# Batch statistics from per-sample moments and a Gram matrix, worked on as 39x39 tables and spread over the partitions by masked matmuls

## Chip, cores, metric

One core of one Trainium2 chip. The metric is device time in microseconds (us), the slowest core of a run, lower is better. Each time is a median over four or five runs. A verdict of "faster" or "slower" needs 2%.

In the lines of the profile PE is TensorE (matmuls) and PEld its weight loads, DVE is VectorE, ACT ScalarE, POOL GpSimd and SP SyncE; a q behind a name is the engine's queue of instructions, L139 is line 139 of that run's kernel, and x4 counts instructions. SBUF and PSUM are on-chip memories; the matmuls here write to PSUM. A load is issued by an engine's queue and has landed when its data is there. Cuts are marked with "...".

## The reference

Shortened (the last two lines leave out reshapes):

```python
B, F0, F1, E, C = (256, 39, 39, 16, 1)          # the inputs really have 1024 samples
rows, cols = np.tril_indices(39, k=-1)          # 741 pairs, col < row
cross = xj[:, rows, :, None] * xi[:, cols, None, :]            # [1024, 741, 16, 16]
mean = jnp.mean(cross, axis=(0, 2, 3), keepdims=True)          # one number a pair
var = jnp.mean(jnp.square(cross - mean), axis=(0, 2, 3), keepdims=True)
normed = (cross - mean) * jax.lax.rsqrt(var + 1e-05) * gamma + beta
out = normed[:, :, None] * W                                   # 777 MB of float32
```

The output takes nearly all the time. The statistics, two numbers for each of 741 pairs, must be known before the first output row.

## The kernel before

The batch lies on the partitions (128 x 8 samples). Mean and variance of each field over E are taken per sample; then all 741 pair products are formed per sample and averaged over the batch by matmuls with a matrix of ones, which also leaves the result on every partition.

```python
for t0 in range(0, NT, TS):                      # TS = 2, NT = 8
    for x, m, v in ((xj_sb, ma, va), (xi_sb, mb, vb)):
        nc.vector.tensor_reduce(ms[:, :, :, 0], xs, AX.X, ALU.add)
        nc.vector.tensor_scalar_mul(ms, ms, 1.0 / E)
        nc.vector.tensor_tensor(dev, xs, ms.to_broadcast([P, TS, F, E]), ALU.subtract)
        nc.scalar.activation(dev, dev, AF.Square)
        nc.vector.tensor_reduce(vs[:, :, :, 0], dev, AX.X, ALU.add)
        # ... scale
q_c = pairs(nc.gpsimd, va, sb, "q_c")            # 38 instructions each, [128, 8, 741] in all
q_a = pairs(nc.vector, ma, mb, "q_a")
batch_mean(ps_m, [q_a], True, True)              # matmuls of 371 and 370 columns
q_b = pairs(nc.vector, sa, vb, "q_b")
batch_mean(ps_v, [q_b, q_c], True, False)
# ... (q_a - mean) ** 2, batch_mean once more, then rsqrt, s and t on [128, 741]
```

The product loop that follows is the same text in both kernels:

```python
for r in order:                                  # 1, 38, 2, 37, ... 
    for t0 in range(0, NT, nt):
        nc.gpsimd.tensor_tensor(xs, xi_sb[...], s_sb[...], ALU.mult)
        # y = xs (outer) xj: VectorE for r <= 6, else 16 ScalarE activations a sample
        # y = (y + t) * W: one VectorE scalar_tensor_tensor a pair
        nc.sync.dma_start(out_v[...], y)
```

## Time and profile before

| | before | changed |
|---|---|---|
| time, first measurement | 3103.19 us | 3065.15 us |
| time, second measurement of both, in one job | 3101.28 us | 3062.89 us |
| first outer product on ScalarE (Z), first profile | 115.56 us | 76.07 us |
| first outer product, second profile | 114.25 us | 75.81 us |
| loop from Z to the end, second profile | 2984.55 us | 2985.09 us |

Z is the moment where the statistics end for the loop; the span minus Z is the loop.

### The profile page before, as it was taken

The page shows a single profiled execution, that of the slowest core. Times are in us where ns is not written, and L with a number is a line of the kernel's source. Part 1 is how long each engine was busy: PE and PEld are TensorE (multiplying, and loading weights), DVE is VectorE, ACT ScalarE, POOL GpSimd, SP SyncE. Part 2 cuts the span into 40 slices and gives each one's busy share as a digit, 9 for nine tenths or more (in the row PEclk, how much of TensorE's full clock was granted, in tenths as well). Part 3 has the DMA queues.
Part 4 walks back from the last instruction along what each step waited for, and adds up shares of the span by engine and source line. Part 5 has one row for each costly group of instructions (what it writes and reads, how often), then busy time and mean ns, then how long its engine had stood idle before and what let it go on. Part 6 is the DMA issues. An engine that isn't in the chain of part 4 may idle for free.

```text
span 3100.0 us, 10969 instructions
## 1 busy us (share of the span) xinstructions
PE 45.6 (1%) x128; PEld 26.7 (1%) x128; DVE 2448.0 (79%) x5253; ACT 2015.7 (65%) x4117; POOL 1659.1 (54%) x252
## 2 busy tenths in 40 slices
PE   2300000000000000000000000000000000000000
PEld 1100000000000000000000000000000000000000
DVE  8687888888888787777777787768777777778786
ACT  2446455464635777777676767676868686868685
POOL 2375757665666656555646464646363636362623
PEclk9655555555555555555555555555555555555555
DMA  2165656566555656666656656565656565666666
GB/s 78 78 265 228 282 244 259 250 269 271 250 252 248 293 237 281 256 268 268 288 249 263 265 240 272 246 281 242 270 243 281 244 281 249 276 263 268 275 267 275
DMA packets 43653, 783.71 MB, mean 253 GB/s; under 512 B 3472, under 2 KB 4496, under 8 KB 11824
## 3 DMA queue, kind: packets, MB, share of 16 engines
q1 hardware_dynamic: 42784, 779.56, 59.1%
q10 hardware_dynamic: 576, 2.56, 0.2%
q0 software_dynamic: 208, 0.89, 0.1%
q14 instruction: 84, 0.69, 0.1%
q8 instruction: 1, 0.02, 0.0%
HBM read 6.00 MB, written 776.99 MB: 253 GB/s over the span
## 4 chain that ended last, share of the span: by engine, by line
ACT 48%; POOL 45%; DVE 3%; issue 2%; PE 1%; DMA 0%; POOLq 0%; DVEq 0%; ACTq 0%
ACT y L183 48%; POOL xs L166 45%; PE ps_v L111 1%; DVE y L191 1%; DVE q_a L100 1%; DVE dev L86 0%; PE ps_m L111 0%; DMA xj_sb<-in_r_xj_dram 0%; DVE ma L83 0%; DVE vb L88 0%; DVE va L88 0%; DVE mb L83 0%; DVE inv L140 0%; DVE rstd L146 0%; DVE inv L144 0%
## 5 line engine op out<-in xcount | busy, mean ns | idle before, releaser
L191 DVE SCALAR_TENSOR_TENSOR y<-y,t_sb,w_sb 128x256 f32<-128x256 f32 (+2 forms) x5068 | 2314.6, 534 | 610.3 <-ACT y L183 610.1
L183 ACT ACTIVATE y<-xs,xj_sb 128x608 f32<-128x608 f32 (+31 forms) x4096 | 1994.9, 580 | 978.7 <-POOL xs L166 978.7
L166 POOL TENSOR_TENSOR xs<-xi_sb,s_sb 128x576 f32<-128x576 f32 (+19 forms) x206 | 1637.3, 7958 | 1368.8 <-ACT y L183 1315.6
L175 DVE TENSOR_TENSOR y<-xs,xj_sb 128x256 f32<-128x256 f32 (+5 forms) x48 | 51.5, 1136 | 1.5 <-POOL xs L166 1.4
L100 POOL TENSOR_TENSOR q_c<-va,sb 128x8 f32<-128x8 f32 (+37 forms) x38 | 19.6, 553 | 39.3 <-DVE sb L93 39.3
L87 ACT ACTIVATE dev<-dev 128x1248 f32<-128x1248 f32 x8 | 9.9, 1243 | 26.1 <-DVE dev L86 25.9
L129 ACT COPY mean<-ps_m 128x371 f32<-128x371 f32 (+1 forms) x2 | 0.9, 468 | 31.0 <-PE ps_m L111 31.0
L138 DVE TENSOR_SCALAR var<-ps_v 128x371 f32<-128x371 f32 (+1 forms) x2 | 1.1, 545 | 22.1 <-PE ps_v L111 22.0
L100 DVE TENSOR_TENSOR q_a<-ma,mb 128x8 f32<-128x8 f32 (+37 forms) x38 | 18.2, 554 | 0.0
L142 ACT ACTIVATE rstd<-inv 128x741 f32<-128x741 f32 x1 | 0.8, 822 | 25.9 <-DVE inv L140 25.9
L111 PE MATMUL ps_m<-q_a,ones 128*128 128x371 f32 (+1 forms) x32 | 15.7, 662 | 56.1 <-DVE q_a L100 56.1
L83 DVE TENSOR_REDUCE ma<-xj_sb 128x78 f32<-128x1248 f32 x4 | 5.8, 1452 | 6.9 <-DMA xj_sb<-in_r_xj_dram 6.9
L111 PE MATMUL ps_v<-q_a,ones 128*128 128x371 f32 (+1 forms) x32 | 10.2, 474 | 0.0
L111 PE MATMUL ps_v<-q_b,ones 128*128 128x371 f32 (+1 forms) x32 | 10.2, 474 | 0.0
L111 PE MATMUL ps_v<-q_c,ones 128*128 128x371 f32 (+1 forms) x32 | 10.1, 474 | 0.0
L100 DVE TENSOR_TENSOR q_b<-sa,vb 128x8 f32<-128x8 f32 (+37 forms) x38 | 9.9, 341 | 0.0
L111 PEld LDWEIGHTS ps_m<-q_a,ones 128*128 128x128 f32 x32 | 8.5, 274 | 62.7 <-issue 57.0
L131 DVE TENSOR_TENSOR q_a<-q_a,mean 128x741 f32<-128x741 f32 x8 | 6.8, 925 | 1.6 <-ACT mean L129 1.6
L132 ACT ACTIVATE q_a<-q_a 128x741 f32<-128x741 f32 x8 | 6.6, 822 | 1.1 <-DVE q_a L131 1.0
L111 PEld LDWEIGHTS ps_v<-q_a,ones 128*128 128x128 f32 x32 | 6.1, 189 | 3.9
L111 PEld LDWEIGHTS ps_v<-q_c,ones 128*128 128x128 f32 x32 | 6.1, 189 | 3.9
L111 PEld LDWEIGHTS ps_v<-q_b,ones 128*128 128x128 f32 x32 | 6.1, 189 | 3.9
(30 smaller groups left out, 49.6 us busy)
## 6 DMA issues: line engine op xcount, KB each, us to landing
out_dram<-y SPq DMA_DIRECT2D x14, 4608.0 KB, 12.4
out_dram<-y SPq DMA_DIRECT2D x15, 4096.0 KB, 11.2
out_dram<-y SPq DMA_DIRECT2D x12, 4864.0 KB, 12.9
out_dram<-y SPq DMA_DIRECT2D x12, 4352.0 KB, 11.8
out_dram<-y SPq DMA_DIRECT2D x14, 3584.0 KB, 10.0
out_dram<-y SPq DMA_DIRECT2D x15, 3072.0 KB, 8.8
out_dram<-y SPq DMA_DIRECT2D x12, 3840.0 KB, 10.6
out_dram<-y SPq DMA_DIRECT2D x12, 3328.0 KB, 9.3
```

The source lines that it names most:

```text
L83: nc.vector.tensor_reduce(ms[:, :, :, 0], xs, AX.X, ALU.add)
L87: nc.scalar.activation(dev, dev, AF.Square)
L100: engine.tensor_tensor(q[:, :, first[r] : first[r] + r], rows[:, :, r : r + 1].to_broadcast([P, NT, r]), cols[:, :, 0:r], ALU.mult,)
L111: nc.tensor.matmul(acc[:, : n1 - n0], ones, q[:, t, n0:n1], start=start and k == 0, stop=stop and k == len(qs) * NT - 1,)
L129: nc.scalar.copy(mean[:, 0, n0:n1], acc[:, : n1 - n0])
L131: nc.vector.tensor_sub(q_a[:, t], q_a[:, t], mean[:, 0])
L132: nc.scalar.activation(q_a[:, t], q_a[:, t], AF.Square)
L138: nc.vector.tensor_scalar_add(var[:, n0:n1], acc[:, : n1 - n0], BN_EPS)
L166: nc.gpsimd.tensor_tensor(xs, xi_sb[:, t0 : t0 + nt, 0:r, :], s_sb[:, :, n0 : n0 + r, :].to_broadcast([P, nt, r, E]), ALU.mult,)
L175: nc.vector.tensor_tensor(y[:, t], xs[:, t].unsqueeze(2).to_broadcast([P, r, E, E]), xj_sb[:, t0 + t, r : r + 1, :].unsqueeze(3).to_broadc ...
L183: nc.scalar.activation(y[:, t, :, i, :], xs[:, t], AF.Copy, scale=xj_sb[:, t0 + t, r, i : i + 1],)
L191: nc.vector.scalar_tensor_tensor(y2[:, :, c, :], y2[:, :, c, :], t_sb[:, n0 + c : n0 + c + 1], w_sb.to_broadcast([P, nt, EE]), ALU.add, AL ...
```

## The change

The intent is to make the statistics stage short: fewer matmul columns, arithmetic on 39x39 tables instead of 128x741, and subtracts shared with GpSimd. It takes per-sample sums of each field, and squares about a common shift (the field's mean over 256 samples, two of the eight on each partition), so that nothing large cancels. A Gram matrix by matmul then gives every pair's moments at once. Cut to its core:

```diff
-        nc.gpsimd.dma_start(g_sb, gamma.partition_broadcast(P))
-        nc.gpsimd.dma_start(b_sb, beta.partition_broadcast(P))
+        for r in range(1, F):                       # 38 + 38 loads of 4 to 152 bytes
+            nc.sync.dma_start(g_sq[r : r + 1, 0:r], gamma[n0 : n0 + r].unsqueeze(0))
+            nc.scalar.dma_start(b_sq[r : r + 1, 0:r], beta[n0 : n0 + r].unsqueeze(0))
+        def shifts():   # matmul of the first sums with ones, then
+            nc.scalar.activation(shift..., ps_s[:, 0 : 2 * F], AF.Copy, scale=k_s)
+        def squares(t0):
+                engine = nc.vector if (t0, x) in DEV_ON_VECTOR else nc.gpsimd   # 3 of 8 on VectorE
+                engine.tensor_tensor(dev, src[...], shift..., ALU.subtract)
+                nc.scalar.activation(dev, dev, AF.Square, scale=0.25)
+                nc.vector.tensor_reduce(to, dev, AX.X, ALU.add)
+                nc.vector.scalar_tensor_tensor(to, total[...], 1.0 / E, shift..., ALU.mult, ALU.subtract)
+        def gram(t0):
+            for t in range(t0, t0 + TS):
+                for acc, lhs in zip(ps_g, (fa[:, t, 0], fa[:, t, 1], ones[:, 0:F])):
+                    nc.tensor.matmul(acc[0:F, 0 : 2 * F + 1], lhs, fb[:, t], ...)
-        (114 pair products, three batch means, all arithmetic on [128, 741])
+        (22 instructions on [39, 39] tables, giving stq = s and t)
+        for r0, r1 in ROW_GROUPS:                   # 7 groups of up to 6 rows
+            nc.vector.tensor_tensor(wide, stq (n times), eye[:, r0:r1], ALU.mult)   # [39, n * 78]
+            nc.tensor.matmul(ps, ones[0:F, :], wide, start=True, stop=True)
+            for r in range(r0, r1):
+                nc.scalar.copy(st_sb[:, :, first[r] : first[r] + r], ps[:, r - r0, :, 0:r])
```

More of the change, by code (lines that the diff above doesn't have):

```diff
@@ L15 @@
 VECTOR_ROW = 6
+DEV_ON_VECTOR = ((2, 1), (4, 1), (6, 1))
+ROW_GROUPS = ((1, 7), (33, 39), (7, 13), (27, 33), (13, 19), (21, 27), (19, 21))
 @with_exitstack
@@ L43, in tile_pair_outer_batchnorm @@
     NP = F * (F - 1) // 2
-    H0 = (NP + 1) // 2
-    halves = ((0, H0), (H0, NP))
     first = [r * (r - 1) // 2 for r in range(F)]
@@ L51, in tile_pair_outer_batchnorm @@
     w_sb = cpool.tile([P, 1, EE], F32, name="w_sb")
-    s_sb = cpool.tile([P, 1, NP, 1], F32, name="s_sb")
-    t_sb = cpool.tile([P, NP], F32, name="t_sb")
+    st_sb = cpool.tile([P, 2, NP], F32, name="st_sb")
+    s_sb = st_sb[:, 0:1].unsqueeze(3)
+    t_sb = st_sb[:, 1]
     xi_v = xi.rearrange("(p t) f e -> p t f e", t=NT)
@@ L64, in tile_pair_outer_batchnorm @@
     with tc.tile_pool(name="stat", bufs=1) as st, tc.tile_pool(
-        name="dev", bufs=2
-    ) as devp, tc.tile_pool(name="ps", bufs=1, space=bass.MemoryType.PSUM) as psp:
-        g_sb = st.tile([P, NP], F32, name="g_sb")
-        b_sb = st.tile([P, NP], F32, name="b_sb")
+        name="dev", bufs=3
+    ) as devp, tc.tile_pool(name="ps", bufs=1, space=bass.MemoryType.PSUM) as psp, tc.tile_pool(
+        name="psx", bufs=3, space=bass.MemoryType.PSUM
+    ) as psx:
         nc.gpsimd.dma_start(w_sb[:, 0, :], w.rearrange("o i j -> (o i j)").partition_broadcast(P))
-        nc.gpsimd.dma_start(g_sb, gamma.partition_broadcast(P))
-        nc.gpsimd.dma_start(b_sb, beta.partition_broadcast(P))
-        ones = st.tile([P, P], F32, name="ones")
-        nc.gpsimd.memset(ones, 1.0 / NB)
-        ma = st.tile([P, NT, F, 1], F32, name="ma")
-        mb = st.tile([P, NT, F, 1], F32, name="mb")
-        va = st.tile([P, NT, F, 1], F32, name="va")
-        vb = st.tile([P, NT, F, 1], F32, name="vb")
-        for t0 in range(0, NT, TS):
-            for x, m, v in ((xj_sb, ma, va), (xi_sb, mb, vb)):
-                xs, ms, vs = x[:, t0 : t0 + TS], m[:, t0 : t0 + TS], v[:, t0 : t0 + TS]
-                nc.vector.tensor_reduce(ms[:, :, :, 0], xs, AX.X, ALU.add)
-                nc.vector.tensor_scalar_mul(ms, ms, 1.0 / E)
-                dev = devp.tile([P, TS, F, E], F32, tag="dev", name="dev")
-                nc.vector.tensor_tensor(dev, xs, ms.to_broadcast([P, TS, F, E]), ALU.subtract)
-                nc.scalar.activation(dev, dev, AF.Square)
-                nc.vector.tensor_reduce(vs[:, :, :, 0], dev, AX.X, ALU.add)
-                nc.vector.tensor_scalar_mul(vs, vs, 1.0 / E)
-        ma, mb, va, vb = (x[:, :, :, 0] for x in (ma, mb, va, vb))
-        sa = st.tile([P, NT, F], F32, name="sa")
-        sb = st.tile([P, NT, F], F32, name="sb")
-        nc.vector.tensor_mul(sb, mb, mb)
-        nc.vector.tensor_mul(sa, ma, ma)
-        nc.vector.tensor_add(sa, sa, va)
-        def pairs(engine, rows, cols, name):
-            q = st.tile([P, NT, NP], F32, name=name)
-            for r in range(1, F):
-                engine.tensor_tensor(
-                    q[:, :, first[r] : first[r] + r],
-                    rows[:, :, r : r + 1].to_broadcast([P, NT, r]),
-                    cols[:, :, 0:r],
-                    ALU.mult,
-                )
-            return q
-        def batch_mean(ps, qs, start, stop):
-            for k, (q, t) in enumerate((q, t) for q in qs for t in range(NT)):
-                for acc, (n0, n1) in zip(ps, halves):
-                    nc.tensor.matmul(
-                        acc[:, : n1 - n0],
-                        ones,
-                        q[:, t, n0:n1],
-                        start=start and k == 0,
-                        stop=stop and k == len(qs) * NT - 1,
-                    )
-        q_c = pairs(nc.gpsimd, va, sb, "q_c")
-        q_a = pairs(nc.vector, ma, mb, "q_a")
-        ps_m = [psp.tile([P, 512], F32, name=f"ps_m{h}") for h in range(2)]
-        ps_v = [psp.tile([P, 512], F32, name=f"ps_v{h}") for h in range(2)]
-        batch_mean(ps_m, [q_a], True, True)
-        q_b = pairs(nc.vector, sa, vb, "q_b")
-        batch_mean(ps_v, [q_b, q_c], True, False)
-        mean = st.tile([P, 1, NP], F32, name="mean")
-        for acc, (n0, n1) in zip(ps_m, halves):
-            nc.scalar.copy(mean[:, 0, n0:n1], acc[:, : n1 - n0])
-        for t in range(NT):
-            nc.vector.tensor_sub(q_a[:, t], q_a[:, t], mean[:, 0])
-            nc.scalar.activation(q_a[:, t], q_a[:, t], AF.Square)
-        batch_mean(ps_v, [q_a], False, True)
-        var = st.tile([P, NP], F32, name="var")
-        for acc, (n0, n1) in zip(ps_v, halves):
-            nc.vector.tensor_scalar_add(var[:, n0:n1], acc[:, : n1 - n0], BN_EPS)
-        inv = st.tile([P, NP], F32, name="inv")
@@ new lines, in tile_pair_outer_batchnorm @@
+        g_sq = st.tile([F, F], F32, name="g_sq")
+        b_sq = st.tile([F, F], F32, name="b_sq")
+        nc.vector.memset(g_sq, 0.0)
+        nc.vector.memset(b_sq, 0.0)
+        for r in range(1, F):
+            n0 = first[r]
+            nc.sync.dma_start(g_sq[r : r + 1, 0:r], gamma[n0 : n0 + r].unsqueeze(0))
+            nc.scalar.dma_start(b_sq[r : r + 1, 0:r], beta[n0 : n0 + r].unsqueeze(0))
+        ones = st.tile([P, P], F32, name="ones")
+        nc.gpsimd.memset(ones, 1.0)
+        eye = st.tile([F, F], F32, name="eye")
@@ new lines, in tile_pair_outer_batchnorm @@
+        nc.gpsimd.affine_select(
+            out=eye, in_=ones[0:F, 0:F], compare_op=ALU.is_equal, fill=0.0, base=0,
+            pattern=[[-1, F]], channel_multiplier=1,
+        )
+        total = st.tile([P, NT, 2, F], F32, name="total")
+        fa = st.tile([P, NT, 2, F], F32, name="fa")
+        fb = st.tile([P, NT, 2 * F + 1], F32, name="fb")
+        nc.gpsimd.memset(fb[:, :, 2 * F : 2 * F + 1], 1.0)
+        shift = st.tile([P, 2, F], F32, name="shift")
+        shift_r = st.tile([F, 1], F32, name="shift_r")
@@ new lines, in tile_pair_outer_batchnorm, with sums @@
+        ps_s = psp.tile([P, 512], F32, name="ps_s")
+        ps_r = psp.tile([P, 512], F32, name="ps_r")
+        ps_g = [psp.tile([P, 512], F32, name=f"ps_g{k}") for k in range(3)]
+        k_s = 1.0 / (TS * P * E)
+        def sums(t0):
+            for x, src in enumerate((xj_sb, xi_sb)):
+                nc.vector.tensor_reduce(
+                    total[:, t0 : t0 + TS, x], src[:, t0 : t0 + TS], AX.X, ALU.add
+                )
+        def shifts():
+            for t in range(TS):
+                nc.tensor.matmul(
+                    ps_s[:, 0 : 2 * F],
+                    ones,
+                    total[:, t].rearrange("p x f -> p (x f)"),
+                    start=t == 0,
+                    stop=t == TS - 1,
+                )
+            for t in range(TS):
+                nc.tensor.matmul(
+                    ps_r[0:F, 0:1], total[:, t, 0], ones[:, 0:1], start=t == 0, stop=t == TS - 1
+                )
+            nc.scalar.activation(
+                shift.rearrange("p x f -> p (x f)"), ps_s[:, 0 : 2 * F], AF.Copy, scale=k_s
+            )
+            nc.scalar.activation(shift_r, ps_r[0:F, 0:1], AF.Copy, scale=k_s)
@@ new lines, in squares @@
+        def squares(t0):
+            for x, src in enumerate((xj_sb, xi_sb)):
+                dev = devp.tile([P, TS, F, E], F32, tag="dev", name="dev")
+                engine = nc.vector if (t0, x) in DEV_ON_VECTOR else nc.gpsimd
+                engine.tensor_tensor(
+                    dev,
+                    src[:, t0 : t0 + TS],
+                    shift[:, x : x + 1, :].unsqueeze(3).to_broadcast([P, TS, F, E]),
+                    ALU.subtract,
+                )
+                nc.scalar.activation(dev, dev, AF.Square, scale=0.25)
+                to = fa[:, t0 : t0 + TS, 1] if x == 0 else fb[:, t0 : t0 + TS, F : 2 * F]
+                nc.vector.tensor_reduce(to, dev, AX.X, ALU.add)
+                to = fa[:, t0 : t0 + TS, 0] if x == 0 else fb[:, t0 : t0 + TS, 0:F]
+                nc.vector.scalar_tensor_tensor(
+                    to,
+                    total[:, t0 : t0 + TS, x],
+                    1.0 / E,
+                    shift[:, x : x + 1, :].to_broadcast([P, TS, F]),
+                    ALU.mult,
+                    ALU.subtract,
+                )
@@ new lines, in gram @@
+        def gram(t0):
+            for t in range(t0, t0 + TS):
+                for acc, lhs in zip(ps_g, (fa[:, t, 0], fa[:, t, 1], ones[:, 0:F])):
+                    nc.tensor.matmul(
+                        acc[0:F, 0 : 2 * F + 1], lhs, fb[:, t], start=t == 0, stop=t == NT - 1
+                    )
+        sums(0)
+        shifts()
+        for t0 in range(0, NT, TS):
+            squares(t0)
+            if t0 + TS < NT:
+                sums(t0 + TS)
+            gram(t0)
+        g1 = st.tile([F, 2 * F + 1], F32, name="g1")
@@ new lines, in tile_pair_outer_batchnorm @@
+        g2 = st.tile([F, 2 * F + 1], F32, name="g2")
+        g3 = st.tile([F, 2 * F + 1], F32, name="g3")
+        for to, acc in zip((g1, g2, g3), ps_g):
+            nc.scalar.activation(to, acc[0:F, 0 : 2 * F + 1], AF.Copy, scale=1.0 / NB)
+        e_ab, e_abb, e_a = g1[:, 0:F], g1[:, F : 2 * F], g1[:, 2 * F : 2 * F + 1]
+        e_aab, e_aabb, e_aa = g2[:, 0:F], g2[:, F : 2 * F], g2[:, 2 * F : 2 * F + 1]
+        e_b, e_bb = g3[:, 0:F], g3[:, F : 2 * F]
+        u, v = shift_r, shift[0:F, 1, :]
@@ new lines, in tile_pair_outer_batchnorm, with small @@
+        stt = nc.vector.scalar_tensor_tensor
+        def small(name):
+            return st.tile([F, F], F32, name=name)
+        k, q1, q2, var, rstd, inv = (small(n) for n in ("k", "q1", "q2", "var", "rstd", "inv"))
+        stq = st.tile([F, 2, F], F32, name="stq")
+        mean = small("mean")
+        stt(k, e_b, u, e_ab, ALU.mult, ALU.add)
+        stt(k, v, e_a, k, ALU.mult, ALU.add)
+        stt(mean, v, u, k, ALU.mult, ALU.add)
+        stt(q1, e_bb, u, e_abb, ALU.mult, ALU.add)
+        nc.vector.tensor_add(q1, q1, e_abb)
@@ L140, in tile_pair_outer_batchnorm @@
+        stt(q1, q1, u, e_aabb, ALU.mult, ALU.add)
+        stt(q2, e_ab, u, e_aab, ALU.mult, ALU.add)
+        nc.vector.tensor_scalar_mul(q2, q2, 2.0)
+        stt(q2, v, e_aa, q2, ALU.mult, ALU.add)
+        nc.vector.tensor_mul(q2, q2, v)
+        nc.vector.tensor_add(q1, q1, q2)
+        nc.vector.tensor_mul(k, k, k)
+        nc.vector.tensor_sub(q1, q1, k)
+        nc.vector.tensor_scalar(var, q1, 0.0, BN_EPS, ALU.max, ALU.add)
         nc.vector.reciprocal(inv, var)
-        rstd = st.tile([P, NP], F32, name="rstd")
@@ L146, in tile_pair_outer_batchnorm @@
         nc.vector.tensor_mul(rstd, rstd, inv)
-        s2 = s_sb[:, 0, :, 0]
-        nc.vector.tensor_mul(s2, rstd, g_sb)
-        nc.vector.tensor_mul(t_sb, mean[:, 0], s2)
-        nc.vector.tensor_sub(t_sb, b_sb, t_sb)
+        nc.vector.tensor_mul(stq[:, 0], rstd, g_sq)
+        nc.vector.tensor_mul(mean, mean, stq[:, 0])
+        nc.vector.tensor_sub(stq[:, 1], b_sq, mean)
+        for r0, r1 in ROW_GROUPS:
+            n = r1 - r0
+            wide = devp.tile([F, n, 2 * F], F32, tag="wide", name="wide")
+            nc.vector.tensor_tensor(
+                wide,
+                stq.rearrange("p x f -> p (x f)").unsqueeze(1).to_broadcast([F, n, 2 * F]),
+                eye[:, r0:r1].unsqueeze(2).to_broadcast([F, n, 2 * F]),
+                ALU.mult,
+            )
+            ps = psx.tile([P, n, 2, F], F32, tag="ps", name="ps")
+            nc.tensor.matmul(
+                ps.rearrange("p r x f -> p (r x f)"),
+                ones[0:F, :],
+                wide.rearrange("p r f -> p (r f)"),
+                start=True,
+                stop=True,
+            )
+            for r in range(r0, r1):
+                nc.scalar.copy(st_sb[:, :, first[r] : first[r] + r], ps[:, r - r0, :, 0:r])
     order = []
```

## The prediction

> **What bounds the kernel now.** I read the page's list of costly groups first, then the chain that ended last in order of time, then the DMA issues. The page of the kernel before:
>
> ```profile
> L191 DVE SCALAR_TENSOR_TENSOR y<-y,t_sb,w_sb 128x256 f32<-128x256 f32 (+2 forms) x5068 | 2314.6, 534 | 610.3 <-ACT y L183 610.1
> L183 ACT ACTIVATE y<-xs,xj_sb 128x608 f32<-128x608 f32 (+31 forms) x4096 | 1994.9, 580 | 978.7 <-POOL xs L166 978.7
> L166 POOL TENSOR_TENSOR xs<-xi_sb,s_sb 128x576 f32<-128x576 f32 (+19 forms) x206 | 1637.3, 7958 | 1368.8 <-ACT y L183 1315.6
> ```
>
> Nearly everything is the product loop: VectorE scales rows (L191), waits for ScalarE's outer products (L183), which wait for GpSimd's xs (L166). The change doesn't touch that loop. It rewrites only what comes ahead of it, so I read the chain of the first 260 us piece by piece (columns: start us, length us, what):
>
> ```profile
> 0.74 6.10 DMA xj_sb<-in_r_xj_dram
> ...
> 42.82 18.09 DVE q_a L100 x38
> ...
> 60.95 10.80 PE ps_m L111 x24
> 71.76 29.98 PE ps_v L111 x96
> ...
> 102.34 4.80 DVE inv L140
> ...
> 112.51 3.02 POOL xs L166 x2
> 115.54 0.02 issue
> 115.56 13.99 ACT y L183 x21
> ```
>
> The reader is to see the statistics stage as one serial stretch. Loading ends at 6.84. VectorE's per-field moments fill 6.87 to 42.8, the pair products 18.1, the matmuls over 741 columns 10.8 + 30.0, the arithmetic over 741 columns 10.7 (101.8 to 112.5), and ScalarE starts its first outer product at **115.56**. I call that moment Z. All after it, 3100.0 - 115.6 = 2984 us, is the loop.
>
> **What the Trainium skill says.** (1) "SBUF — State Buffer", "Who interferes with whom": a VectorE instruction with two SBUF inputs and a GpSimd instruction that reads SBUF lock each other out, the later blocks fully; `tensor_reduce` does not contend. The trace agrees on the first: with a batch of L191 running, a GpSimd xs waits it out, and one beside no such work takes 1.2 to 1.5 us. On the reduce no run shows it yet.
>
> ```profile
> 126.89 1.46 POOL L166 TENSOR_TENSOR xs<-xi_sb,s_sb 128x608 f32<-128x608 f32 x1 [5.26 <-ACT y L183]
> 137.96 37.26 POOL L166 TENSOR_TENSOR xs<-xi_sb,s_sb 128x608 f32<-128x608 f32 x2 [9.62 <-ACT y L183]
> ```
>
> (2) "DMA: Bandwidth & Descriptors", "Anatomy of one DMA": a transfer has a fixed cost of about 2 us, mostly completion, and any semaphore wait happens on the issuing sequencer. The trace fits: from the two rows below, (12.9 - 7.6) us over 2304 KB is 2.3 us per 1000 KB, which leaves 7.6 - 5.9 = 1.7 us fixed. (3) "ScalarE: Activation LUTs", "What ACT_TABLE_LOAD costs": an ACTIVATE with immediates takes 186 ns + 0.833 ns an element, and back-to-back ones overlap by 93 ns. The trace agrees: 186 + 1040 = 1226 ns for 1248 elements, measured 1243.
>
> ```profile
> out_dram<-y SPq DMA_DIRECT2D x12, 4864.0 KB, 12.9
> out_dram<-y SPq DMA_DIRECT2D x14, 2560.0 KB, 7.6
> xi_sb<-in_r_xi_dram ACTq DMA_DIRECT2D x4, 624.0 KB, 13.1
> L87 ACT ACTIVATE dev<-dev 128x1248 f32<-128x1248 f32 x8 | 9.9, 1243 | 26.1 <-DVE dev L86 25.9
> L87 ACT ACT_TABLE_LOAD x1 | 1.3, 1283 | 3.0 <-issue 3.0
> L83 DVE TENSOR_REDUCE ma<-xj_sb 128x78 f32<-128x1248 f32 x4 | 5.8, 1452 | 6.9 <-DMA xj_sb<-in_r_xj_dram 6.9
> ```
>
> **Part 1: what goes.** The pair products (114 instructions on VectorE and GpSimd), 128 matmuls of 371 columns and all arithmetic on 128x741. The matmuls become 24 of 79 columns into a 39-row Gram table, plus 4 for the shift; the arithmetic runs on 39x39. From the end of the moments (42.8) to Z the old kernel spends 72.7 us; most of that goes.
>
> **Part 2: what comes, up to the shift.** Here I see a cost that the intent does not mention. gamma and beta are now loaded row by row into a 39x39 square: 38 tiny DMAs on SyncE's queue and 38 on **ScalarE's**. In the compiled order all 38 of ScalarE's issues stand ahead of its first table load and of the shift, from which every later step follows. They share four semaphores: issue k waits for the landing of issue k-4, and the first four wait for the four xi loads. The last xi load is issued at 2.1 us, and the longest takes 17.2 us to land (view of xi_sb's instructions), so issue 4 goes at about 19.3. Then rounds of four, each one landing time. I take 2.1 us (1.7 fixed, plus wait and issue; an issue alone took 0.33 to 0.46 us, so four take less than a round): issue 36 at 19.3 + 8 x 2.1 = 36.1, issue 38 about 1 us later, 37.1, the table load 1.3. So ScalarE makes the shift at **T0 = 38.4 us**. VectorE's eight sums of the raw inputs (8 x 1.36 = 10.9 us from 6.87, ends 17.8, or a little later with the last load) lie beside this and cost nothing. So do SyncE's 38.
>
> **Part 3: from the shift to the Gram tables.** Per pair of inputs: subtract (GpSimd five times, VectorE three), square on ScalarE (1.24), reduce on VectorE (1.36 apart). GpSimd's subtract has 1248 elements; an xs of 608 took about 1.2 us alone, so 2.4 us, an estimate. In the compiled order: three GpSimd subtracts end at T0 + 7.3, the third square at 8.6, its reduce at 10.1; VectorE's two subtracts 12.9; three reduces 17.0; the last GpSimd subtract has waited for its buffer (15.7) and ends 18.1; square, reduce 20.8; VectorE's last subtract 22.1; square 23.4; reduce **24.9**. The six Gram matmuls left and the three copies out of PSUM: about 2.2, so 27.1.
>
> **Part 4: tables and spreading.** Some 22 dependent VectorE instructions on 39 elements at about 0.2 us (a 128x78 one takes 0.20 in the trace): 4.4; reciprocal 39 x 6.5 ns + 0.1 = 0.35 (from 4.79 us for 741), square root with its two hand-overs 0.4; its second table load of 1.3 lies beside VectorE's chain. That is 32.3. First wide product 39x468: 0.6. Seven matmuls of up to 468 columns: an unwarmed one of 371 took 0.66, so 0.8 each and about 5.2 for all. The 38 copies to the final rows come to 38 x 0.1 + 0.833 ns x 1482 = 5.0 us and run beside the matmuls, about 1 us behind. So **Z = T0 + 40**. GpSimd's xs of rows 1 and 38 need only the first two groups' copies, so they should be ready.
>
> **Sum.** Z = 38.4 + 40 = 78.4, against 115.6: 37.2 us less. The loop starts with the same state (two xs ready, no y in flight), so I carry its 2984 us over unchanged: 3103.07 - 37.2 = **3066 us**, ratio 0.988.
>
> **Rivals.** *A: the tiny DMAs do not hold ScalarE.* If they land as they are issued, the shift comes at about 13 us, and the stage is then paced by subtracts and squares: Z about 55 to 60, the time about 3045. For it: the intent is a short stage, and SyncE's issues do no harm. Against: the waits are in the compiled order, in front of the table load. Even then the gain stays under 2%. *B: small transfers are much slower than the fixed 1.7 us* (they write rows under 512 bytes, and two queues compete): 3.5 us a round gives T0 = 50 and 3077; the gain shrinks to 26 us. *C: the loop changes its rhythm.* It runs in batches of three rows of a sample because GpSimd slips one xs in just as VectorE's batch starts (126.89) and is then locked out for 36 us. A different phase at the start could lose that slot; a batch of two would cost 20.7 us a sample against 19.2 for 38-pair rows (10.6 us of ScalarE, then 15.4 us a sample on VectorE), up to 7%. Against: the slot is taken at every batch of the trace that I looked at, whatever the row length, and the first batch starts from the same buffers. I give a changed rhythm 4%. *D: the shared port* between GpSimd's subtracts and VectorE's two-input work stretches part 3 by some 3 us.
>
> **Range and chances.** T0 from 34 to 46 and the rest from 37 to 47 give Z from 71 to 90 and times from 3059 to 3078; rival A widens the low side: **3054 to 3078**. Faster by over 2% would need Z below 53.5, hardly reachable with a shift before 13 and 40 us behind it: 3%. Slower by over 2% only by a changed rhythm: 1%. Within 2%: 96%.
>
> **What would show it.** Right: ScalarE's first ACTIVATE (the shift copy) near 38 us with its queue's DMA issues ahead of it about 0.5 us apart on average; GpSimd and VectorE idle between 18 and 38; the last moment reduce some 25 us after the shift; first outer product near 78; the loop from there 2984 us within 5. Wrong: shift near 13 us (A), rounds over 3 us (B), or a loop length off by over 15 us (C), seen in how many xs wait through a whole batch.

## The result

The changed kernel takes 3065.15 us (3064.97 to 3065.37, 4 runs) against 3103.19 us: ratio 0.988, interval 0.986 to 0.989. A ratio is the mean time of one kernel's runs over the mean of the other's in the same rounds, so not quite the ratio of these medians. 3066 us were predicted.

The chain of the changed kernel in order of time (start us, length us, what), first profile. Its pieces stand where pair products, batch means and wide arithmetic stood before:

```profile
31.78 6.91 POOL dev L128 x3
...
42.19 2.31 POOL dev L128
...
48.63 2.32 POOL dev L128
...
57.95 1.55 PE ps_g L151 x10
...
62.40 0.41 DVE inv L200
...
65.42 9.74 PE ps L221 x12
...
76.07 22.31 ACT y L261 x32
```

The gain is the shift of the last line, from 115.56 to 76.07. The whole profile was taken again for both kernels: there Z moves from 114.25 to 75.81, 38.4 us, and the time from 3101.28 to 3062.89, also 38.4 us. The loop differs by 0.5 us.

By pieces in the first profile: the moments end 15.1 us later than before (57.9 instead of 42.8), because the shift comes so late, and all from there to Z takes 18.2 us instead of 72.7.

Two views show what the total hides. First the timeline of ScalarE's queue and engine (start, length, queue or engine, line, operation, then the idle time before it and what ended it):

```profile
0.81 2.30 ACTq L62 DMA_DIRECT2D xi_sb<-in_r_xi_dram  x4
7.49 22.64 ACTq L77 DMA_DIRECT2D b_sq<-in_L_rec_beta_dram  x38
30.16 1.28 ACT L119 ACT_TABLE_LOAD   x1 [30.16 <-DMA b_sq<-in_L_rec_beta_dram]
31.46 0.24 ACT L119 ACTIVATE shift<-ps_s 128x78 f32<-128x78 f32 x1
```

The shift's matmul was done at 11.3 us. ScalarE copies its result 20 us later, because 38 issues and the table load stand in front. The first four of these issues start at 7.49, 11.86, 14.92 and 17.91 us: in the compiled order they reuse the semaphores of the four input loads, and wait for them. The other 34 take 12.0 us. Then VectorE's timeline from there:

```profile
31.73 0.24 DVE L139 SCALAR_TENSOR_TENSOR fa<-total,shift 128x78 f32<-128x78 f32 x1 [11.15 <-ACT shift_r L122]
31.88 2.35 DVE L139 SCALAR_TENSOR_TENSOR fb<-total,shift 128x78 f32<-128x78 f32 x1
34.16 2.35 DVE L139 SCALAR_TENSOR_TENSOR fa<-total,shift 128x78 f32<-128x78 f32 x1
36.44 2.35 DVE L139 SCALAR_TENSOR_TENSOR fb<-total,shift 128x78 f32<-128x78 f32 x1
38.71 0.23 DVE L139 SCALAR_TENSOR_TENSOR fa<-total,shift 128x78 f32<-128x78 f32 x1
```

Eight equal instructions should take 0.23 us each. Three of them take 2.35 us, each ending within 0.1 us of one of GpSimd's three subtracts (34.14, 36.41 and 38.69). Busy time is not always work.

### The profile page after: what moved, and what is told of

Its sections match the earlier page's. It is cut to its first block, busy times and chain, and to the rows that moved or that the text cites. A ratio compares the mean times of both kernels' runs of the same rounds, so it can differ in the third digit from the quotient of the medians.

```text
span 3063.6 us, 10861 instructions
## 1 busy us (share of the span) xinstructions
PE 18.7 (1%) x70; PEld 11.9 (0%) x70; DVE 2408.1 (79%) x5174; ACT 2017.1 (66%) x4150; POOL 1647.3 (54%) x219
## 4 chain that ended last, share of the span: by engine, by line
ACT 48%; POOL 46%; issue 3%; DVE 1%; DMA 1%; PE 0%; POOLq 0%; DVEq 0%; ACTq 0%
ACT y L261 48%; POOL xs L244 46%; DVE y L269 1%; POOL dev L128 0%; PE ps L221 0%; DMA out_dram<-y 0%; DMA xj_sb<-in_r_xj_dram 0%; ACT dev L135 0%; PE ps_g L151 0%; DVE fb L137 0%; DVE fa L137 0%; DVE dev L128 0%; POOLq L244 0%; ACT st_sb L229 0%; DVE wide L214 0%
## 5 line engine op out<-in xcount | busy, mean ns | idle before, releaser
L269 DVE SCALAR_TENSOR_TENSOR y<-y,st_sb,w_sb 128x256 f32<-128x256 f32 (+2 forms) x5068 | 2314.5, 534 | 613.0 <-ACT y L261 612.8
L244 POOL TENSOR_TENSOR xs<-xi_sb,st_sb 128x576 f32<-128x576 f32 (+19 forms) x206 | 1634.4, 7944 | 1345.9 <-ACT y L261 1320.1
L128 POOL TENSOR_TENSOR dev<-xj_sb,shift 128x1248 f32<-128x1248 f32 x4 | 9.3, 2326 | 36.9 <-ACT shift_r L122 29.2
L221 PE MATMUL ps<-wide,ones 39*128 39x468 f32 (+1 forms) x14 | 10.2, 921 | 5.7 <-DVE wide L214 5.7
L221 PEld LDWEIGHTS ps<-wide,ones 39*128 39x128 f32 x14 | 4.5, 329 | 11.3 <-DVE wide L214 6.4
L151 PEld LDWEIGHTS ps_g<-fb,fa 128*39 128x39 f32 x32 | 4.3, 182 | 42.3 <-issue 31.2
```

The lines of the kernel that those rows point to most:

```text
L128: engine.tensor_tensor(dev, src[:, t0 : t0 + TS], shift[:, x : x + 1, :].unsqueeze(3).to_broadcast([P, TS, F, E]), ALU.subtract,)
L151: nc.tensor.matmul(acc[0:F, 0 : 2 * F + 1], lhs, fb[:, t], start=t == 0, stop=t == NT - 1)
L221: nc.tensor.matmul(ps.rearrange("p r x f -> p (r x f)"), ones[0:F, :], wide.rearrange("p r f -> p (r f)"), start=True, stop=True,)
L244: nc.gpsimd.tensor_tensor(xs, xi_sb[:, t0 : t0 + nt, 0:r, :], s_sb[:, :, n0 : n0 + r, :].to_broadcast([P, nt, r, E]), ALU.mult,)
L269: nc.vector.scalar_tensor_tensor(y2[:, :, c, :], y2[:, :, c, :], t_sb[:, n0 + c : n0 + c + 1], w_sb.to_broadcast([P, nt, EE]), ALU.add, AL ...
```

## The experiments

Seven runs, all correct, five rounds each beside the kernel before. They came on different chips, so I compare by Z and the shift time from the profiles, and by ratios to the kernel before. Z of the changed kernel differs by 0.26 us between its two profiles.

| | time | ratio | shift copied at | Z |
|---|---|---|---|---|
| changed (repeat) | 3062.89 | 0.9878 | 31.20 | 75.81 |
| beta on SyncE | 3045.68 | 0.9820 | 11.58 | 59.50 |
| shift from PSUM | 3059.52 | 0.9866 | 31.12 | 72.76 |
| narrow spread | 3058.33 | 0.9862 | 31.32 | 71.56 |
| all three | 3039.01 | 0.9799 | 11.44 | 52.59 |
| all three, GpSimd | 3037.15 | 0.9795 | 11.49 | 50.47 |
| before (repeat) | 3101.28 | 1.0002 | | 114.25 |

### Beta's loads off ScalarE's queue

```diff
-            nc.scalar.dma_start(b_sq[r : r + 1, 0:r], beta[n0 : n0 + r].unsqueeze(0))
+            nc.sync.dma_start(b_sq[r : r + 1, 0:r], beta[n0 : n0 + r].unsqueeze(0))
```

> One edit to the changed kernel: beta's 38 tiny loads go on SyncE's queue beside gamma's, none on ScalarE's. Theory (the issues in front of ScalarE's shift delay the whole stage): ScalarE's shift copy moves from 31.5 us to about 11.4 us, right behind the shift matmul; VectorE still has to take its sums of the later loads in between, so the first outer product starts near 59 us instead of 76.1 and the time is about 3048 us. Rival (the stage is paced by something else, for instance the last input load, or 76 issues on one queue that then arrive too late for the gamma and beta step): the shift is early, but the first outer product stays above 70 us and the time above 3059 us.

Measured: 3045.68 us, Z 59.50. ScalarE's timeline in this run:

```profile
11.58 0.24 ACT L119 ACTIVATE shift<-ps_s 128x78 f32<-128x78 f32 x1 [7.15 <-PE ps_s L108]
...
14.24 1.24 ACT L135 ACTIVATE dev<-dev 128x1248 f32<-128x1248 f32 x1 [2.38 <-POOL dev L128]
```

The wait in front of the shift is now the matmul. The shift comes 19.6 us earlier, but Z only 16.3 us: VectorE has sums of the later loads to do in between, which used to lie in the wait. SyncE issues eight of the 76 loads as the inputs land, the others from 18.5 us on, mostly one every 0.295 us, and is done at 38.9, and the step that needs them follows at 47 us without a wait. So the 38 issues on ScalarE's queue cost the changed kernel 16.3 us net. That is shown; how much of it is the wait for the input loads and how much the issues behind it, this run doesn't part.

### The shift read from PSUM

```diff
+        mean_w = st.tile([P, P], F32, name="mean_w")
+        nc.gpsimd.memset(mean_w, k_s)
-                    ones,                                   # weights of the shift matmul
+                    mean_w,
-                    shift[:, x : x + 1, :].to_broadcast([P, TS, F]),
+                    ps_s[:, x * F : x * F + F].unsqueeze(1).to_broadcast([P, TS, F]),
             # ... ScalarE's copy of the shift drops its scale
```

> One edit to the changed kernel: the eight small instructions (total/E - shift) read the shift from PSUM, where a matmul by a constant leaves it already scaled, so they have one SBUF input instead of two. GpSimd's subtracts still read the copy in SBUF. Theory (the small two-input instructions are locked out while GpSimd subtracts, three of them 2.35 us each, and this stands on the path): they take about 0.25 us each, VectorE's first reduce starts some 4 us after the shift instead of 7.9, the next subtract gets its buffer earlier, and the first outer product starts 2 to 3 us earlier: about 3062.5 us. Rival (GpSimd's three subtracts set the pace anyway, or the port isn't the reason): under 0.7 us of gain.

Measured: 3059.52 us, Z 72.76, so 3.0 us less. The same four instructions, from VectorE's timeline:

```profile
31.39 0.24 DVE L141 SCALAR_TENSOR_TENSOR fa<-total,ps_s 128x78 f32<-128x78 f32 x1 [11.09 <-ACT shift_r L124]
31.54 0.23 DVE L141 SCALAR_TENSOR_TENSOR fb<-total,ps_s 128x78 f32<-128x78 f32 x1
31.69 0.23 DVE L141 SCALAR_TENSOR_TENSOR fa<-total,ps_s 128x78 f32<-128x78 f32 x1
31.84 0.23 DVE L141 SCALAR_TENSOR_TENSOR fb<-total,ps_s 128x78 f32<-128x78 f32 x1
...
35.07 1.45 DVE L139 TENSOR_REDUCE fa<-dev 128x78 f32<-128x1248 f32 x1 [2.42 <-ACT dev L137]
```

GpSimd's subtracts are unchanged (6.87 us for three). With one SBUF input VectorE's instruction is not locked out; with two it is. The "SBUF — State Buffer" page of the Trainium skill, "Who interferes with whom", says just this of a GpSimd instruction that reads SBUF, and this run and the changed kernel are its two sides: 0.23 against 2.35 us. In both runs VectorE's reduces run beside GpSimd's subtracts at their usual 1.44 us, which agrees with what that section says of them.

### Narrow columns

```diff
+            c = r1 - 1
-            wide = devp.tile([F, n, 2 * F], F32, tag="wide", name="wide")
+            wide = devp.tile([F, n, 2, c], F32, tag="wide", name="wide")
             # the product, the PSUM tile and the matmul follow this shape
```

> One edit to the changed kernel: the wide products and their matmuls take only the columns that a group of rows needs (the row number of its longest row, twice) instead of all 78, 1664 columns in all instead of 2964. Theory (the seven matmuls, 9.7 us on the path at the granted clock of 0.5, are paid by the column): the matmuls take about 5.7 us instead of 10.2, the first outer product starts about 4 us earlier, the time is about 3061 us. Rival (they are paid by the instruction, or ScalarE's 38 copies are as long): under 1 us of gain.

Measured: 3058.33 us, Z 71.56, so 4.25 us less. Groups of matmuls by shape (count, busy us, mean ns), first in the changed kernel, then in this one:

```profile
L221 PE MATMUL ps<-wide,ones 39*128 39x468 f32 x12 | 9.7, 997 | 5.7 <-DVE wide L214 5.7
...
L221 PE MATMUL ps<-wide,ones 39*128 39x156 f32 x2 | 0.7, 464 | 0.0
```

```profile
L222 PE MATMUL ps<-wide,ones 39*128 39x456 f32 x2 | 1.9, 1045 | 0.0
L222 PE MATMUL ps<-wide,ones 39*128 39x384 f32 x2 | 1.5, 844 | 0.0
...
L222 PE MATMUL ps<-wide,ones 39*128 39x72 f32 x2 | 0.7, 450 | 5.2 <-DVE wide L215 5.2
```

The matmuls are paid mostly by the column: all of them took 10.24 us for 2964 columns and take 6.29 us for 1664. Another 0.4 us of the gain is the first wide product, 0.65 us before and 0.24 now. Note the count: **one float32 matmul stands as two records in the profile** (six of 468 columns give x12). My expectation named a granted clock of 0.5. In the first profile the record does say 0.50 in this stretch; for the repeat of the changed kernel `prof` prints 1.00, and the chain has the same 9.74 us. The third line is the kernel before, in its long stretch of matmuls:

```profile
65.40:75.20 9.80, 9.79 (x14) 4.42 (x14) 3.73 (x6) 3.33 (x31) 1.89 (x2) 0.50 0.00 1
```

```profile
65.10:74.90 9.80, 9.74 (x13) 4.38 (x14) 3.77 (x7) 3.31 (x30) 1.89 (x2) 1.00 0.00 1
```

```profile
71.70:101.70 30.00, 30.00 (x97) 17.88 (x95) 7.36 (x9) 8.33 (x10) 0.00 (x0) 1.00 0.00 1
```

(Stretches and their length; columns: busy us and count of PE, weight loads, VectorE, ScalarE, GpSimd, then the clock, DMA share, GB/s.) The kernel before took 29.98 us for 96 records of 370 or 371 columns, 0.84 ns a column; the changed kernel takes 9.74 us for 12 records of 468, 1.73 ns a column, twice as much. So 0.50 fits both profiles of the changed kernel. The 1.00 of the repeat is no measurement: its packed trace holds no clock record at all, and `prof` prints 1.00 then. "TensorE: Matmul & The Clock Gate", "Seeing it yourself", warns that the clock records can be unreliable; here they are missing. That page's clock of a cold array, 1.2 GHz ("What's actually happening"), and the four passes of a true float32 matmul that "FP8 and Floating Point Precision" names under "TensorE Precision Notes", two for each record if they split evenly, give 468 x 2 / 1.2 = 780 ns a record, an estimate. The chain's 9.74 us over 12 records make 0.81 us each, with a first start among them.

### All three

```diff
+ the three edits above, nothing else
```

> The three edits together (beta's loads on SyncE's queue, the shift read from PSUM, narrow columns). Theory, if the three costs lie one after the other on one path: 3065.2 - 17 - 2.5 - 4 = about 3041.5 us, first outer product near 52 us. Rival: with an early shift and a shorter chain the 76 tiny loads on one queue land too late for the step that needs gamma and beta, and the time stays near 3046 us or above.

Measured: 3039.01 us, Z 52.59, so 23.2 us before the repeat of the changed kernel; the three edits alone gave 16.3 + 3.05 + 4.25 = 23.6. So the three costs lie one after the other. The loads on SyncE's queue are issued by 38.8 us, the step that uses gamma starts at 44.5, and no wait for them shows. The rival falls.

### Seven of eight subtracts on GpSimd

```diff
-DEV_ON_VECTOR = ((2, 1), (4, 1), (6, 1))
+DEV_ON_VECTOR = ((4, 1),)
-        name="dev", bufs=3
+        name="dev", bufs=4
         # ... and the three edits above
```

> The three edits together, and seven of the eight subtracts on GpSimd with four buffers instead of five with three. In the profile of the three edits VectorE is busy without a gap from 14.6 to 36 us, so two subtracts of 1.37 us each less on it, and no wait for a buffer, should end the moments 3 to 4 us earlier: first outer product near 49 us, 3.5 us less than the three edits alone. Rival: the last of the 76 tiny loads was issued at 38.4 us there, so the step that needs gamma and beta, then due at about 41 us, waits for them, and the gain stays under 2 us.

Measured: 3037.15 us, Z 50.47: 2.1 us less than with the three edits, not 3.5. The reason is not the rival's, since the step that needs gamma starts at 42.4 us without a wait. VectorE's one subtract left now meets GpSimd's last and waits for it:

```profile
25.45 2.33 POOL L130 TENSOR_TENSOR dev<-xi_sb,shift 128x1248 f32<-128x1248 f32 x1
...
26.05 3.05 DVE L130 TENSOR_TENSOR dev<-xi_sb,shift 128x1248 f32<-128x1248 f32 x1
```

That is 1.6 us over its usual 1.44, the same lock as before, in a new place, and about what is missing of the 3.5; no run took that meeting away, so this reason is read from the trace and not tested. The run changes two things at once, subtracts and buffers, and doesn't part them. This is the shortest time: ratio 0.9795 (0.9782 to 0.9809) to the kernel before.

### The two kernels again

```diff
  (no edit)
```

> The changed kernel unaltered, so that the experiments can be set against it on one chip, and to see whether its product loop is really longer. In its first profile 2987.5 us lie between the first outer product and the end, against 2984.4 in the kernel before and 2984.7 to 2985.1 in the first four experiments, whose loop is the same. If this belongs to that one run, the loop here is 2984.5 to 2985.5 us and ScalarE's rows of 16 products take as long as in the kernel before; if it belongs to the changed kernel, it is about 3 us longer again.

> The kernel before unaltered, profiled on the same chip as its rival of this call: first outer product at 115.5 us as in the first profile, loop 2984.4 us within 1 us, ratio 1.

Measured: 3062.89 us (3062.72 to 3063.05) and 3101.28 us (3100.59 to 3101.59). The loop is 2985.09 us with the change and 2984.55 us without, so the 3 us extra in the changed kernel's first profile don't belong to the change. ScalarE's busy time in the loop was 1999.12 us there, 1994.89 us in the repeat, and 1994.87 and 1994.91 us in the two profiles of the kernel before, for the same instructions. It was not one odd run: all four runs of the changed kernel in that first job took 3064.97 to 3065.37 us, 2 us more than in the repeat, and the kernel before took 3102.97 to 3104.05 us in it, also some 2 us more. Why that job was slower, these runs don't tell. Z of the kernel before was 114.25 and not 115.5: its pair products ended the same (60.95), but its first batch mean took 9.21 us instead of 10.80. The clock record there (65 to 70 us) says 1.00 in this profile and 0.78 in the first, which agrees.

## Why the prediction was right

The time was right to 1 us, and the order of events was as told. That it came so close was luck: several errors of some us cancelled.

- **The loop is carried over.** Right: 2984.55 and 2985.09 us on the same chip. Rival C (another rhythm) falls: GpSimd's extra xs slips in at 87.42 us in the changed kernel, 11.35 us after Z, as it did at 126.89 before, 11.33 us after Z, and the next one waits the same 36 us.
- **The tiny loads hold ScalarE.** The mechanism was right and is shown by the first experiment. Its size was off: predicted T0 38.4 us, measured 31.46. The fourth issue came at 17.9 us instead of 19.3 (1.4 us), and the 34 issues behind it took 12.0 us to the start of the last instead of 17.8 (5.8 us): one each 0.35 us, four in 1.4 us. I had taken 2.1 us for four, from a fixed cost that I fitted to output transfers of megabytes and to the "about 2 us" of "DMA: Bandwidth & Descriptors", "Anatomy of one DMA". In the compiled order a queue has four semaphores, so four in 1.4 us means that a load of this size is landed, or at least no longer waited for, in 1.4 us or less. Whether landing or issuing sets the 0.35 us is open: one queue alone, with eight semaphores, issued mostly every 0.295 us in the first experiment, but there both the queue's rival and the semaphores had changed.
- **From the shift to Z**: predicted 40, measured 76.07 - 31.46 = 44.6. Two terms were mis-sized. The moments took 26.4 us to the last reduce instead of 24.9, although subtracts, squares and reduces were each as estimated: the lock of the shared port, which I had named as rival D (3 us) and not put in the sum. The second experiment takes it away and gains 3.0 us; the moments then take 23.5 us, so without the lock my 24.9 was 1.4 too long. The other term: the spread took 10.65 us from the first matmul to Z, where I had 7.1 (5.2 for the matmuls, about 1 for the copies behind them, and 0.9 for which no term is given). The matmuls alone took 10.24. I read 0.66 us in the row of the old kernel as the cost of a matmul, and multiplied by seven. It is the cost of a record, and each float32 matmul has two. The old page showed this: its code has 64 of these matmuls, its row of counts 128, and I wrote "128 matmuls" without asking. The Gram matmuls with their copies (1.9 us against 2.2) and the table arithmetic (59.78 to 64.72, 4.9 us against 5.2) were right.
- **Sum**: I put the shift 7 us too late and made what follows 4.6 us too short, so Z came at 76.1 instead of 78.4. The loop of that profile was 3.1 us longer than carried over, and the kernel before's time lay 3.1 us above its profile's span, the changed one's 1.8; together these make up the rest.
- **Slips that changed nothing**: T0 up to 46 and the rest up to 47 make Z up to 93, not 90. In rival C, 10.6 and three times 15.4 us make 18.9 us a sample, not 19.2; the trace has a batch of three every 58.5 us.
- **Rival A** (ScalarE not held) was put at "Z about 55 to 60, the time about 3045". This is what the first experiment makes of it, 59.5 and 3045.7. As a forecast for the change it was wrong. **Rival B** (slower loads) was wrong in direction.

So a rewrite of the stage took some 38 us out of 115, and the loop's 2985 us keep that under 2%. The experiments took out 25 us more (Z from 75.81 to 50.47); 16 of those had gone to 38 small loads in front of the wrong engine.

## What to carry to other kernels

DMA issues on a compute engine's queue stand in line with that engine's instructions (moving them brought the shift from 31.2 to 11.6 us): put none ahead of an instruction from which a whole stage follows, and put many small ones on a queue whose engine computes nothing. A VectorE instruction with two SBUF inputs waits for the end of the GpSimd subtract that it meets (here 0.23 us became 2.35, and 1.44 became 3.05); one input in PSUM freed it. When a sum comes out right, check its terms one by one: here errors of 7 and 4.6 us cancelled, and only the experiments gave each cost its own size.

## What the Trainium skill lacked or had wrong

- "DMA: Bandwidth & Descriptors", "Anatomy of one DMA": its fixed cost of about 2 us a transfer is fitted to another path (GpSimd's descriptors), as its heading says, and was too long for loads of 4 to 152 bytes from SyncE and ScalarE: with four semaphores a queue, one went out every 0.35 us on each queue, so four in 1.4 us; a single queue with eight semaphores issued one mostly every 0.295 us. The same page's "Latency and other measured facts" has a least time of about 800 ns for tiny transfers, which the prediction passed over and which these 1.4 us don't contradict. A rate for many small loads in a row is in neither section.
- "SBUF — State Buffer", "Who interferes with whom": the cases looked at here agree, also that one SBUF input is free of the lock. It has the rule (the loser waits for the whole instruction) but no measured case of a small VectorE instruction: 0.23 us became 2.35 us beside a subtract of 2.3 us, and was 0.23 us again with the other input in PSUM.
- "TensorE: Matmul & The Clock Gate" doesn't say that a float32 matmul stands in the profile as two records, each with its weight load (six matmuls, x12).
- The same page, "Seeing it yourself", warns that clock records can be unreliable, but not that a profile can lack them: four of the nine profiles here hold none and print 1.00, and in three of these the same matmuls took the same 9.74 us as under a record of 0.50.
